# A four-sequence decoder layer on one core: a recorded order with shifted keys, a rule that keeps VectorE's two-tile steps and GpSimd's products apart, and two products moved to VectorE

## The chip, the cores and the metric

The kernel runs on one core of one Trainium2 chip. The metric is the device time of one execution in microseconds (us); before the change it is 1579.58 us, the median of three runs (1576.39 to 1582.81). The core has TensorE (PE; its weight loads are listed as PEld), VectorE (DVE), ScalarE (ACT), GpSimd (POOL) and SyncE (SP, which here only issues DMAs).

## The reference, cut to what matters

For B = 4 sequences of S = 512 tokens and 512 features, in float32, three blocks follow each other; each adds to the residual and is normalised:

```python
# 1 differential attention: 16 query heads in 8 pairs, 8 key heads in 4 groups, D = 128
p = softmax(q1 @ k1.T * D**-0.5, causal) - lam * softmax(q2 @ k2.T * D**-0.5, causal)
o = rmsnorm(p @ v) * subln_w * (1 - LAMBDA_INIT)        # v has 256 columns
x = layernorm(x + o.reshape(B, S, 1024) @ out_w.T + out_b)

# 2 a selective scan over a second input ctx (512 inner channels, 16 states)
u  = silu(causal_conv4(ctx @ in_proj.T) + conv_b)
dt = softplus(dt_proj(x_proj(u)[:16]) + dt_b);  Bm, Cm = x_proj(u)[16:]
state = state * exp(dt * A) + (dt * u) * Bm             # for each of the 512 steps
y  = (sum_n(state * Cm) + D * u) * silu(x)
x = layernorm(x + y.T)

# 3 a shared GLU and 16 routed experts on a 128-wide latent, 8 experts per token
shared = (x @ sw1.T * relu(x @ swg.T)**2) @ sw2.T
xl = x @ Wdown.T
acc = sum_e w[:, e] * ((xl @ rw1[e].T * relu(xl @ rwg[e].T)**2) @ rw2[e].T)
x = layernorm(x + shared + acc @ Wup.T)
```

Attention and the scan of a sequence don't need each other until block 2 multiplies by silu(x): the scan's input is ctx.

## The kernel before, in words

**Recording and ordering.** The kernel doesn't issue its instructions as it goes. `Notes` records every operation of every engine as a `Step` with a `key` (a due time in us that the code sets by hand as `nc.key = ...`), a cost, a lag and the steps that it depends on. `Notes.order` then lets a list of five engines run through these steps: at each event, each free engine takes, of its ready steps, the one with the smallest key, if its key is within `window` of the oldest step that is still open and its buffers are free. An ACT step that needs another function table has 10 added to its rank. The order that comes out is issued with the scheduler of the framework switched off, by one line in `Notes.trace`; this is why all instructions of the profile carry the same line, L325. On the chip each engine works through its own list in that order and waits at semaphores; the keys and costs decide the order alone.

**Vector steps beside GpSimd.** Before the change the ordering allows for an overlap of the two engines as a slowdown: a vector step that `shares` (over 256 columns and two tiles in SBUF) is made longer by a quarter of its overlap with a GpSimd `tensor_tensor`.

**Attention.** There are 16 units n (4 groups x 4 sequences), with keys from `t_unit(n) = 40 + 73.8 n`. A unit projects kT (`ps_qk` from `wk`), v (`ps_v`, evicted by VectorE, which adds the bias) and two pairs of queries (`ps_qk` from `wq`). For each of two heads and four row tiles, `softmax` makes scores `s` on PE, VectorE masks them and takes the row extreme (`e`, `nm`), ScalarE takes exp with its sum (`e`), VectorE forms `cf` and subtracts the second map from the first (`e<-e,cf`); `values` transposes (`pt`), copies (`pT`), and multiplies by v (`po`). After four tiles the output is scaled by an RMS (`rs`, a power taken on GpSimd), transposed (`pt_o`, `oT`) and projected (`ps_out`); VectorE adds the result to `res[b]`. At the start GpSimd adds the output bias to the four `res[b]` (four operations of 128x2048).

**The scan.** `scan(b)` projects ctx (`ps_in`), convolves on ScalarE and VectorE (`y`), multiplies by a sigmoid (`sgc`), projects (`ps_x`, `ps_dt`), takes the softplus in several steps (`du`, `lo`, `dt`: five 1024-column vector operations and one of the tensor-scalar kind for each half of the channels), and then takes 16 states x 2 halves. Each of these 32 steps per sequence is a vector product `h<-du,bc`, two exps on ScalarE (`da`), the hardware scan `h<-da,h`, a vector product `h<-h,bc`, and a DMA from the GpSimd queue that adds h to y in DRAM. The keys are `t_scan = SCAN + PACE * (16 b + n)`. PE does almost nothing for it, so it lies beside attention.

**Experts.** `experts(b)` loads y, forms the gate `sg` (sigmoid on ScalarE, times x on GpSimd, then `yb` times `sg` on VectorE), transposes (`pt_y`) and adds to `res[b]`, normalises, transposes (`pt_x`, `x2T`), routes (`ps_gate`, `pr`, `pt_w`), makes the latent `xl` (`ps_lat`) and the shared GLU (`pg_s`, `ph_s`). For each of 16 experts GpSimd makes `xw = xl * wb` (the latent scaled by the token's weight for that expert), and for each of two halves PE makes `pg` and `ph`, ScalarE relu and square, VectorE `ht = relu * ph`, and PE adds into `pa`. Then `ps_y`, the residual and the last normalisation.

## Time and profile before

| quantity | value |
|---|---|
| runs | 1582.81, 1579.58, 1576.39 us |
| the profiled execution | 1578.32 us, span 1576.3 us |
| granted TensorE clock, mean | 0.991 |
| PE | 1546.2 us busy (98%), 4944 instructions |
| DVE | 1159.6 us busy (74%), 1956 instructions |
| ACT | 953.2 us busy (60%), 2084 instructions |
| POOL | 307.0 us busy (19%), 288 instructions |
| DMA | 196.18 MB moved, mean 124 GB/s |

Every float32 matmul of the program is two passes of PE in the profile and every transpose one: 2112 matmuls and 720 transposes make 4944 instructions. The ends of passes are modelled in the profile, and a pass's listed duration overlaps the next pass, so times on PE are better read from start to start: a busy share of 98% doesn't say that PE ran at its peak for 98% of the span.

### The profile page before, as it was taken

The page shows a single profiled execution, that of the slowest core. Times are in us where ns is not written, and L with a number is a line of the kernel's source. Part 1 is how long each engine was busy: PE and PEld are TensorE (multiplying, and loading weights), DVE is VectorE, ACT ScalarE, POOL GpSimd, SP SyncE. Part 2 cuts the span into 40 slices and gives each one's busy share as a digit, 9 for nine tenths or more (in the row PEclk, how much of TensorE's full clock was granted, in tenths as well). Part 3 has the DMA queues.
Part 4 walks back from the last instruction along what each step waited for, and adds up shares of the span by engine and source line. Part 5 has one row for each costly group of instructions (what it writes and reads, how often), then busy time and mean ns, then how long its engine had stood idle before and what let it go on. Part 6 is the DMA issues. An engine that isn't in the chain of part 4 may idle for free.

```text
span 1576.3 us, 15893 instructions
## 1 busy us (share of the span) xinstructions
PE 1546.2 (98%) x4944; PEld 848.5 (54%) x4944; DVE 1159.6 (74%) x1956; ACT 953.2 (60%) x2084; POOL 307.0 (19%) x288
## 2 busy tenths in 40 slices
PE   7899999999999999999999999999999999999998
PEld 3465665556656555565555556655445445445443
DVE  4888897899889789988889998898883423423323
ACT  3765566686566668666565866775854444444443
POOL 4111121111121110121111121232331321320221
PEclk9899999999999999999999999999999999999999
DMA  8366683557568355666745567564771442341341
GB/s 276 90 127 118 120 165 93 107 143 133 97 131 198 65 123 120 134 111 146 168 75 123 125 147 160 118 130 94 178 162 60 138 133 78 116 128 55 118 122 53
DMA packets 105523, 196.18 MB, mean 124 GB/s; under 512 B 10896, under 2 KB 45712, under 8 KB 105440
## 3 DMA queue, kind: packets, MB, share of 16 engines
q1 hardware_dynamic: 87008, 128.06, 29.3%
q0 software_dynamic: 18432, 67.12, 24.9%
q8 instruction: 39, 0.64, 0.2%
q14 instruction: 44, 0.36, 0.1%
HBM read 119.25 MB, written 75.89 MB: 124 GB/s over the span
## 4 chain that ended last, share of the span: by engine, by line
PE 92%; DVE 4%; ACT 2%; issue 1%; DMA 0%; SPq 0%; POOLq 0%; DVEq 0%
PE ps_qk L325 20%; PE ps_out L325 13%; PE po L325 8%; PE s L325 8%; PE pa L325 7%; PE ph L325 7%; PE ps_v L325 6%; PE pg L325 6%; PE ps_y L325 3%; DVE h L325 2%; PE pt L325 2%; PE ps_in L325 2%; PE pg_s L325 2%; PE ph_s L325 2%; PE pt_o L325 2%
## 5 line engine op out<-in xcount | busy, mean ns | idle before, releaser
L325 DVE TENSOR_TENSOR_SCAN h<-da,h 128x1024 f32<-128x1024 f32 x128 | 296.9, 2319 | 3.4 <-ACT da L325 0.2
L325 POOL DMA_DIRECT2D y<-h x128 | 112.6, 880 | 779.2 <-DVE h L325 508.2
L325 PE MATMUL ps_out<-ow,oT 128*128 128x512 f32 x512 | 241.6, 593 | 0.6 <-DVE res L325 0.6
L325 PE MATMUL ps_qk<-xT,wq 128*128 128x512 f32 x512 | 238.3, 593 | 3.4 <-DVE v L325 2.2
L325 DVE TENSOR_TENSOR ht<-relu,ph 128x512 f32<-128x512 f32 x128 | 87.6, 685 | 176.1 <-ACT relu L325 87.7
L325 ACT ACTIVATE da<-dt,a_neg 128x512 f32<-128x512 f32 (+1 forms) x256 | 175.5, 716 | 33.2 <-DVE h L325 31.1
L325 ACT ACTIVATE relu<-pg 128x512 f32<-128x512 f32 x128 | 76.2, 595 | 165.3 <-PE pg L325 162.5
L325 PE MATMUL s<-kT,qT 128*128 128x384 f32 (+3 forms) x512 | 168.3, 439 | 0.2 <-DVE nm L325 0.2
L325 PE MATMUL po<-v,pT 128*128 128x256 f32 x640 | 161.2, 383 | 1.8 <-ACT pT L325 1.8
L325 DVE TENSOR_TENSOR h<-h,bc 128x1024 f32<-128x1024 f32 x128 | 158.8, 1241 | 1.4
L325 PEld LDWEIGHTS po<-v,pT 128*128 128x128 f32 x640 | 121.5, 191 | 68.7 <-issue 42.0
L325 DVE TENSOR_TENSOR h<-du,bc 128x1024 f32<-128x1024 f32 x128 | 157.8, 1233 | 0.0
L325 ACT ACTIVATE e<-e,nm 128x128 f32<-128x128 f32 (+3 forms) x256 | 141.4, 555 | 22.8 <-DVE nm L325 22.3
L325 POOL TENSOR_TENSOR xw<-xl,wb 128x512 f32<-128x512 f32 x64 | 85.9, 1343 | 285.5 <-PE ph L325 133.0
L325 DVE CUSTOM_DVE_ANT_0 e<-s,mask 128x128 f32<-128x128 f32 (+3 forms) x256 | 117.7, 486 | 25.2 <-PE s L325 24.7
L325 PEld LDWEIGHTS ps_qk<-xT,wq 128*128 128x128 f32 x512 | 92.9, 190 | 80.1 <-issue 70.9
L325 PE MATMUL ph<-xw,w_e 128*128 128x512 f32 x256 | 130.8, 593 | 2.8 <-DVE ht L325 2.8
L325 PEld LDWEIGHTS ps_out<-ow,oT 128*128 128x128 f32 x512 | 91.6, 190 | 77.2 <-issue 65.5
L325 PE MATMUL pg<-xl,w_e 128*128 128x512 f32 x256 | 130.7, 593 | 0.0
L325 PE MATMUL pa<-ht,w_e 128*128 128x512 f32 x256 | 130.3, 594 | 0.0
L325 PE MATMUL ps_v<-wv,xT 128*128 128x256 f32 x512 | 122.1, 380 | 1.2 <-DVE v L325 1.2
L325 PE MATMUL ps_qk<-xT,wk 128*128 128x512 f32 x256 | 121.0, 601 | 0.0
(120 smaller groups left out, 2087.6 us busy)
## 6 DMA issues: line engine op xcount, KB each, us to landing
y<-h POOLq DMA_DIRECT2D x128, 512.0 KB, 8.0
bc<-bc SPq DMA_DIRECT2D x64, 512.0 KB, 6.4
wb<-w SPq DMA_DIRECT2D x64, 256.0 KB, 3.6
xT<-in_xT_dram SPq DMA_DIRECT2D x15, 1024.0 KB, 7.5
w_e<-in_rwgT_dram SPq DMA_DIRECT2D x64, 128.0 KB, 2.2
w_e<-in_rw1T_dram SPq DMA_DIRECT2D x64, 128.0 KB, 2.3
w_e<-in_rw2T_dram SPq DMA_DIRECT2D x64, 128.0 KB, 2.4
wq<-in_wqkvT_dram SPq DMA_DIRECT2D x8, 512.0 KB, 7.3
```

Of the source, the lines that this page charges most:

```text
L325: getattr(getattr(self.nc, s.engine), s.name)(*[get(a) for a in s.args], **{k: get(v) for k, v in s.kw.items()})
```

## The change

Three things change.

1. **The order rule.** `shares` gets another meaning: a vector step with at least two operands in SBUF (at least one for `tensor_scalar`; reciprocal, statistics and max never count), and a GpSimd `tensor_tensor` of more than 4 columns. In `order` such a step isn't taken while another such step, of either engine, is running (`port`). The slowdown by a quarter is gone. The limit on PSUM buffers by due time is gone too (it was wide open before), and `order` takes the keys as an argument and keeps its state in local tables.
2. **The keys.** `SHIFT` adds a constant to the key of every step, by the name of the tile that it writes and the first letter of its engine: 86 of them, from -31 to +24. The base constants move too, `SCAN` from 60.47 to 140.0 above all.
3. **Two products change engine.** The gate product `sg * res` (16 of them) and the latent product `xw = xl * wb` (64) go from GpSimd to VectorE.

```diff
+SHIFT = {
+    "aT.s": 14, "a_neg.s": 8, "a_neg.v": -9, "bc.s": 7, ... "da.s": -1, ... "e.s": 8, "e.v": -1, ... "h.v": -4,
...
+}
@@ note
-        s.shares = columns(out) > 256 and sum(not v.buf.pool.psum for v in ins if columns(v) > 1) > 1
+        if engine == "vector":
+            n = 1 if name == "tensor_scalar" else 0 if name in ("reciprocal", "bn_stats", "bn_aggr", "max") else 2
+            s.shares = n > 0 and sum(not v.buf.pool.psum for v in ins) >= n
+        else:
+            s.shares = engine == "gpsimd" and name == "tensor_tensor" and columns(out) > NT
...
+        to = out.buf.name if isinstance(out, View) else s.bufs[0].name
+        s.key = self.key + SHIFT.get(to.rstrip("0123456789") + "." + engine[0], 0.0)
@@ order
+                    if s.shares and port > now:
+                        continue
...
-                if e == "vector" and best.shares:
-                    end += 0.25 * max(0.0, min(end, sharing) - now)
-                elif e == "gpsimd" and best.name == "tensor_tensor":
-                    sharing = end
+                if best.shares:
+                    port = end
@@ decoder_kernel
-    VALUES = 12.88
-    PROJECT, QUERY, SECOND = -22.47, -16.31, 20.46
-    EXPERT = [-18.73, 110.0, 228.82, 350.0]
+    VALUES = 10.71
+    PROJECT, QUERY, SECOND = -20.55, -16.82, 23.75
+    EXPERT = [-18.73, 110.0, 227.64, 350.0]
...
-    RATE, WEIGHTS, DOWN, SCALED = 5.76, 22.64, 6.95, 6.6
+    RATE, WEIGHTS, DOWN, SCALED = 5.76, 22.64, 6.39, 6.6
...
-    SCAN, PACE, CONV, SOFTPLUS = 60.47, 19.34, 70.44, 19.2
+    SCAN, PACE, CONV, SOFTPLUS = 140.0, 19.34, 70.44, 19.2
@@ experts
-            nc.gpsimd.tensor_tensor(sg, sg, res[b][:, i, :], ALU.mult)
+            nc.vector.tensor_tensor(sg, sg, res[b][:, i, :], ALU.mult)
...
-            nc.gpsimd.tensor_tensor(xw, xl, wb, ALU.mult)
+            nc.vector.tensor_tensor(xw, xl, wb, ALU.mult)
```

The list of each engine is known before the run. PE has the same 2832 steps in another order, VectorE has 80 steps more, GpSimd 80 fewer, and ScalarE's function-table loads go from 38 to 42. Everything else is the same work in another order.

More of the change, by code (lines that the diff above doesn't have):

```diff
@@ L1 @@
-import bisect
 import heapq
@@ L21 @@
 P = 128
-SLACK = 50
+ENGINES = ("tensor", "vector", "scalar", "gpsimd", "sync")
+SHIFT = {
+    "aT.s": 14, "a_neg.s": 8, "a_neg.v": -9, "bc.s": 7, "bq.s": -2, "cw.s": -2, "da.g": -4, "da.s": -1, "db.s": 3,
+    "dt.v": -12, "du.v": 20, "e.s": 8, "e.v": -1, "gb.s": -1, "h.v": -4, "ht.v": -6, "kT.s": 4, "ln_mv.v": -13,
+    "ln_nb.v": -7, "ln_rs.g": -2, "ln_st.v": 9, "ln_ve.v": 1, "lo.v": 9, "ls.v": -5, "lt.s": 6, "m.v": -4, "ms.v":
+    -4, "nlam.v": -11, "o.s": -17, "obb.s": 9, "pT.s": -3, "pa.t": 1, "pg.t": -4, "pg_s.t": -8, "ph.t": 3,
+    "ph_s.t": 3, "po.t": -10, "pr.s": -8, "pr.v": -20, "ps_gate.t": -17, "ps_in.t": -2, "ps_out.t": 5, "ps_v.t":
+    1, "ps_x.t": 11, "ps_y.t": -3, "pt_o.t": 3, "pt_w.t": -8, "pt_x.t": 4, "pt_y.t": -12, "relu.s": 23,
+    "relu_s.s": -4, "res.g": -4, "res.s": 7, "res.v": -2, "rp.v": -16, "rs.g": 6, "rs.v": -12, "sc.v": -2, "sg.s":
+    -5, "sg.v": 4, "sgc.s": 5, "sh.v": 6, "sp.v": 14, "sq.s": 4, "sub.v": -9, "v.v": 2, "w.s": 7, "wT.s": -1,
+    "w_d.s": 4, "w_dt.s": 9, "w_e.s": 24, "w_g.s": 4, "w_in.s": -31, "w_u.s": 1, "w_xp.s": 3, "x2T.s": -13,
+    "xd.s": 9, "xl.s": 3, "xm.g": 2, "xm.s": 1, "xw.v": 2, "y.g": -5, "y.s": 6, "y.v": -5, "yb.s": 6, "yb.v": 5,
+}
 B, S, HID = 4, 512, 512
@@ L139 @@
     __slots__ = (
-        "engine", "name", "args", "kw", "key", "at", "cost", "lag", "fill", "after", "left", "ready", "bufs", "table",
-        "engine_at", "shares",
+        "engine", "name", "args", "kw", "key", "at", "cost", "lag", "fill", "after", "left", "bufs", "table", "shares",
     )
@@ L192, in note @@
         s = Step()
-        s.engine, s.name, s.args, s.kw, s.key, s.at = engine, name, args, kw, self.key, len(self.steps)
+        s.engine, s.name, s.args, s.kw, s.at = engine, name, args, kw, len(self.steps)
         out = kw["out"] if "out" in kw else args[0]
@@ L200, in note @@
         s.table = {AF.Exp: "exp", AF.Sigmoid: "sigmoid", AF.Ln: "ln"}.get(args[2]) if name == "activation" else None
-        s.shares = columns(out) > 256 and sum(not v.buf.pool.psum for v in ins if columns(v) > 1) > 1
+        if engine == "vector":
[3 more added lines that the diff above has]
+            s.shares = engine == "gpsimd" and name == "tensor_tensor" and columns(out) > NT
         s.cost, s.lag, s.fill = cost(engine, name, out, rest, kw)
-        s.after, s.left, s.ready, s.bufs = [], 0, 0.0, []
+        s.after, s.left, s.bufs = [], 0, []
         before = {}
@@ L228, in touch, with order @@
             s.bufs.append(b)
-            b.uses += 1
-    def order(self, window=100.0):
-        engines = ("tensor", "vector", "scalar", "gpsimd", "sync")
-        ready = {e: [] for e in engines}
-        free_at = {e: 0.0 for e in engines}
-        events, ends, done, live = [0.0], [], [], set()
-        queue = sorted(self.steps, key=lambda s: (s.key, s.at))
-        sharing = 0.0
-        front, table, filled, landed = 0, "exp", 0.0, {e: [0.0] * 8 for e in engines}
-        seen = set()
-        for s in self.steps:
-            for b in s.bufs:
-                if id(b) not in seen:
-                    seen.add(id(b))
-                    b.key = s.key
-                    b.due = b.pool.due.setdefault(b.counts[-1], [])
-                    bisect.insort(b.due, b, key=lambda b: b.key)
-        for s in self.steps:
-            s.engine_at = None
-            if not s.left:
+    def order(self, keys, window=100.0):
+        steps, begin, finish, ready_at = self.steps, {}, {}, [0.0] * len(self.steps)
+        left = [s.left for s in steps]
+        ready = {e: [] for e in ENGINES}
+        free_at = dict.fromkeys(ENGINES, 0.0)
+        landed = {e: [0.0] * 8 for e in ENGINES}
+        events, ends, done, live, gone, took = [0.0], [], [], set(), {}, {}
+        queue = sorted(steps, key=lambda s: (keys[s.at], s.at))
+        free, due, uses = {}, {}, {}
+        for s in steps:
+            for b in s.bufs:
+                if b in uses:
+                    uses[b] += 1
+                    continue
+                uses[b] = 1
+                for c in b.counts:
+                    free[b.pool, c] = b.pool.free[c]
+                due.setdefault((b.pool, b.counts[-1]), []).append((keys[s.at], s.at, b))
+            if not left[s.at]:
                 ready[s.engine].append(s)
+        due = {c: [b for *_, b in sorted(d, key=lambda t: t[:2])] for c, d in due.items()}
+        front, table, filled, port = 0, "exp", 0.0, 0.0
         while events:
@@ L257, in order @@
             while ends and ends[0][0] <= now:
-                for b in heapq.heappop(ends)[2].bufs:
-                    b.uses -= 1
-                    if not b.uses:
+                s = heapq.heappop(ends)[2]
+                for b in s.bufs:
+                    uses[b] -= 1
+                    if not uses[b]:
                         for c in b.counts:
-                            b.pool.free[c] += 1
-            for e in engines:
+                            free[b.pool, c] += 1
+                        gone.setdefault((b.pool, b.tag), []).append(s)
+            for e in ENGINES:
                 if free_at[e] > now:
@@ L266, in order @@
                 best, least = None, None
+                most = keys[queue[front].at] + window
                 for s in ready[e]:
-                    if s.ready > now or s.key > queue[front].key + window:
+                    if ready_at[s.at] > now or keys[s.at] > most:
                         continue
@@ L271, in order @@
                         continue
-                    rank = (s.key + (10.0 if s.table not in (None, table) else 0.0), s.at)
+                    if s.shares and port > now:
+                        continue
+                    rank = (keys[s.at] + (10.0 if s.table not in (None, table) else 0.0), s.at)
                     if best is not None and rank >= least:
                         continue
-                    new = [b for b in s.bufs if id(b) not in live]
-                    if all(b.pool.free[b.tag] and b in b.due[: b.pool.free[b.counts[-1]] + SLACK * b.pool.psum] for b in new):
+                    if all(
+                        b in live
+                        or free[b.pool, b.tag]
+                        and (b.pool.psum or b in due[b.pool, b.counts[-1]][: free[b.pool, b.counts[-1]]])
+                        for b in s.bufs
+                    ):
                         best, least = s, rank
@@ L282, in order @@
                 for b in best.bufs:
-                    if id(b) not in live:
-                        live.add(id(b))
+                    if b not in live:
+                        live.add(b)
                         for c in b.counts:
-                            b.pool.free[c] -= 1
-                        b.due.remove(b)
+                            free[b.pool, c] -= 1
+                        due[b.pool, b.counts[-1]].remove(b)
+                        if gone.get((b.pool, b.tag)):
+                            took.setdefault(best.at, []).append(gone[b.pool, b.tag].pop(0))
                 end = now + best.cost
-                if e == "vector" and best.shares:
-                    end += 0.25 * max(0.0, min(end, sharing) - now)
-                elif e == "gpsimd" and best.name == "tensor_tensor":
-                    sharing = end
+                if best.shares:
+                    port = end
                 if best.table not in (None, table):
@@ L301, in order @@
                     landed[e].append(max(landed[e][-1], end + lag))
-                best.engine_at = now
+                begin[best.at], finish[best.at] = now, end + lag
                 free_at[e] = end
                 done.append(best)
-                if queue[front] is best:
-                    while front < len(queue) - 1 and queue[front].engine_at is not None:
-                        front += 1
-                    heapq.heappush(events, now)
+                while front < len(queue) - 1 and queue[front].at in begin:
+                    front += 1
+                heapq.heappush(events, now)
                 heapq.heappush(events, end)
@@ L312, in order, with trace @@
                 for s in best.after:
-                    s.left -= 1
-                    seen = end if s.engine == e and best.name != "dma_start" else end + lag
-                    s.ready = max(s.ready, seen)
-                    heapq.heappush(events, s.ready)
-                    if not s.left:
+                    left[s.at] -= 1
+                    ready_at[s.at] = max(ready_at[s.at], end if s.engine == e and best.name != "dma_start" else end + lag)
+                    heapq.heappush(events, ready_at[s.at])
+                    if not left[s.at]:
                         ready[s.engine].append(s)
+        return done, begin, finish, took
+    def trace(self):
+        done = self.order([s.key for s in self.steps])[0]
         assert len(done) == len(self.steps), "the order does not come to an end"
-        return done
-    def trace(self):
-        for s in self.order():
+        for s in done:
             get = lambda v: v.get() if isinstance(v, View) else v
```

## The prediction

> **What bounds it now.** First the page: which engine is full, and what ended last.

> ```profile
> PE 1546.2 (98%) x4944; PEld 848.5 (54%) x4944; DVE 1159.6 (74%) x1956; ACT 953.2 (60%) x2084; POOL 307.0 (19%) x288
> ...
> PE  7899999999999999999999999999999999999998
> ...
> PE 92%; DVE 4%; ACT 2%; issue 1%; DMA 0%; SPq 0%; POOLq 0%; DVEq 0%
> ```

> PE is the bound, and the change gives it the same work. So the question is what PE loses, and where. From the timeline's start times, a pass follows the one before it by 0.429 us at 512 columns, 0.322 at 384, 0.2155 at 256, 0.1095 at 128 and 0.111 at 16. With 2560, 128, 1280, 848 and 128 passes (the counts of the groups by form) that is 1098.2 + 41.2 + 275.8 + 92.9 + 14.2 = 1522 us. The first pass starts at 5.9 and the last starts 7.5 before the end; 1576.3 - 5.9 - 1522 - 7.5 leaves **41 us lost**: idle time that the page shows, and passes at half rate behind a stall. By stage I get 16.3 (0 to 118 us), 7.9 (to 1024), 15.5 (to 1182) and 1.2 (to the end), by adding each step's excess over its form's step. The windows of these stages:

> ```profile
> 0.00:118.00 118.00, 103.98 (x317) 57.63 (x318) 84.84 (x135) 69.57 (x150) 29.26 (x30) 0.96 0.60 164
> 118.00:1024.00 906.00, 904.26 (x3124) 531.75 (x3123) 798.56 (x1342) 600.55 (x1442) 141.17 (x147) 1.00 0.62 127
> 1024.00:1182.00 158.00, 151.23 (x459) 78.03 (x458) 138.89 (x205) 109.13 (x209) 53.70 (x42) 0.96 0.62 141
> 1182.00:1576.00 394.00, 386.75 (x1049) 181.11 (x1047) 137.29 (x277) 173.90 (x284) 82.86 (x69) 1.00 0.33 100
> ```

> The columns are length, then PE, PEld, DVE, ACT and POOL busy, and the granted clock. The long middle is free of loss with DVE at 88%; the clock falls to 0.96 only in the two stages that lose time; DVE is two thirds empty at the end. Then PE's own waits:

> ```profile
> PE pt L325 <- DVE e L325: 3.3, 1, 3.3
> PE ph L325 <- DVE ht L325: 2.8, 2, 1.9
> PE pt_y L325 <- DVE res L325: 2.4, 3, 0.9
> PE ps_qk L325 <- DVE v L325: 2.2, 1, 2.2
> ```

> All four are DVE being late. The timeline says why for two of them, at 30 us and at 1103 us:

> ```profile
> 27.28 2.44 DVE L325 TENSOR_SCALAR a_neg<-a_neg 128x64 f32<-128x64 f32 x1 [1.99 <-ACT a_neg L325]
> 29.64 4.51 DVE L325 TENSOR_TENSOR nlam<-ls 128x1 f32<-128x1 f32 x1
> ...
> 24.83 18.24 POOL L325 TENSOR_TENSOR res<-res,obb 128x2048 f32<-128x2048 f32 x4 [22.52 <-DMA res<-in_x_dram]
> ...
> 1103.13 1.45 POOL L325 TENSOR_TENSOR xw<-xl,wb 128x512 f32<-128x512 f32 x1
> 1103.14 3.60 DVE L325 TENSOR_TENSOR_SCAN h<-da,h 128x1024 f32<-128x1024 f32 x1
> ```

> A one-column subtraction lasts 4.51 us and ends where GpSimd's second addition ends; a scan that takes 2.32 us in its group takes 3.60 beside `xw`, and the `ht` behind it makes PE wait 1.9 us.

> **Start (16.3 us lost).** 1.7 of it are the first passes at half rate, which stay. 2.4 is the `ps_qk` behind `v`: that eviction stands behind `nlam`. In the new lists the four additions on GpSimd and `a_neg`, `nlam` on DVE keep their places, so I expect `v` at 34.3 us again; but the matmul that waits for it now stands behind 56 passes of 512 and 24 of 256 columns instead of 48 and 16: (8 x 0.429) + (8 x 0.2155) = 5.2 us more work in front, against 2.4. Hidden, with 2.8 to spare. The rest, some 9 us from 57 to 71 us and 1.3 at 96, is softplus: in the timeline DVE runs it in one piece from 49.3 to 61.2 us, and the `e` for which PE waits at 62.2 stands behind. In the new order only half of the `ps_dt` matmuls come early (44 us of PE work from the first pass), the other half at 83, and DVE's first softplus step stands behind the subtraction of the first five score tiles. Walking the new DVE list from PE's 31 us to 60 us with the group means, the transposes find `e` ready 0.6 us or more ahead. I leave 0.8 of small steps and 1.0 for waits that I didn't see: 16.3 - 1.7 - 0.8 - 1.0 = **12.8 us gained**; bounds 9 and 14.

> The first matmul comes later: `w_in` twice and three small loads stand in front of the first half of `cT`, which goes from fifth to sixth on SP, at 0.47 us from issue to issue: **0.5 us lost**.

> **Middle (7.9).** About 4 is in the form of the stream (`ps_dt`, `ps_x`, `ps_lat` follow each other by 0.51 to 0.53 us) and stays. 2.1 are two waits beside softplus at 324 and 882 us. With DVE's new list priced by the group means and set against PE's positions, these go, and one of 0.2 comes at 912. A new danger: scan 0's last products need `h` buffers back from DMAs that take 8.0 us to land, just when the next convolution holds two: up to 2 us. **1.0 gained**, between -2 and 3.

> **Transition (15.5).** GpSimd's 16 `xw` and 4 to 8 `sg` leave. What they cost DVE here: its scans, products and small steps lose 10.8 us over their usual time in this stage. What they cost on DVE: `yb<-yb,sg`, also two SBUF tiles, took 0.68 us undisturbed (mean 0.75), so the 80 products are 55 us in all, and 20 to 28 of them fall here: 14 to 19 us. So DVE has more to do in this stage. The scan adds to that: it now ends at 1150 to 1240 us of PE work instead of 1066 to 1130. By PE position and scaled to its busy time, DVE's work goes from 112 to 116 us in 1000 to 1120, with 44.7 us in the 40 from 1040, and from 45 to 101 in 1120 to 1240. The first overload, where `res` is late for `pt_y` and `pt_x`, shrinks from 5.4 to 4.0 us of backlog; the 7.7 that 1024 to 1063 lost go to 5.7. The second is new, 3.4 to 4.7: I take 4.7. The half-rate passes of 1063 to 1103 (2.2) stay. Of 1103 to 1182 (5.6) the two waits for `ht` and what followed go, 1.5 is left. 5.7 + 4.7 + 2.2 + 1.5 = 14.1, **1.4 gained**, between -9 and 9.

> [...]

> **Last stage (1.2).** DVE has 137 us of work in 394, so the other 50 or so products are hidden; the scan's tail up to 1240 makes DVE 84% full there, as in the middle. **1.0 lost**, up to 6. ScalarE's four more table loads cost 1.28 us each by their group, 5.1 us on an engine that is 60% busy: nothing, or 1.3 if one stands in front of a `pT`. In the timeline the load at 25.69 us starts where ScalarE's step before it ends, and the next step starts at 26.99. [...]

> **Sum.** 12.8 - 0.5 + 1.0 + 1.4 - 1.0 = 13.7. Span 1576.3 - 13.7 = 1562.6; what lies around the span is 2.0 (1578.32 - 1576.3), so 1564.6; the median of the runs is 1.3 above the profiled run: **1566 us**, 0.9% faster. Half a per cent, 7.9 us, is what a measurement of this kernel tells from no change.

> **Rivals.**
> - *The transition gives it back (same).* If DVE stays behind from 1024 to 1142, all three stretches lose what the first lost (7.7 in 39 us): 23 instead of 14.1, gain 4.8, 1575 us. For: 44.7 us of work in 40. [...] 0.17.
> - *Slower.* `ht` behind a scan step. In each of the 64 half-experts of the first two sequences ScalarE squares, DVE multiplies, PE adds, and DVE may be in a 2.32 us scan when `relu` is ready. If PE loses 7.7 per 39 us from 1024 to 1221, that is 38.5 against 15.1: 23.4 more, net 9.7 slower, **1589 us**. It decides from 0.21 us lost per half-expert (13.7 / 64). Against: a list priced in order shows `ht` 1 to 2 us ahead of `pa` after 1110. 0.07.
> - *The port rule does nothing at the start.* It works on the recorder's clock, not the chip's. If `v` is waited for all the same, 2.4 come back: 1568. 0.10.
> - *The transition gets better too.* [...] 0.20.
> - The forecast itself: 0.46.

> Faster holds nearly all of the forecast and two rivals: 0.75; same 0.18; slower 0.07. The range, 1553 to 1575, leaves out the slower case and half of the first rival at the top, and at the bottom a transition at its best bound beside a start at its best.

> **What would show it.** Right: no wait of PE for `v`, `e` or `pT` before 100 us, first stage at 3 to 5 us lost; `nlam` still some 4 us long; no scan over 2.4 us; DVE busy near 1200 us; PE idle near 17 us. Wrong: waits of `pa` for `ht` all through 1060 to 1240, a clock below 0.95 in several slices there, or new waits for `h` near 330 us.

## The result, and the profile after

The changed kernel took 1568.93 us, the median of 15 runs (1562.75 to 1577.64), against 1579.58 us for 15 runs of the kernel before beside it (1576.01 to 1590.58). The ratio is 0.9927, with a 95% interval of 0.9907 to 0.9947: 0.7% faster, where 1566 us (0.9% faster) had been forecast, in a range of 1553 to 1575. The profiled execution took 1571.12 us, with a span of 1569.4; it is 2.2 us above its median, and the profiled execution before is 1.3 below its own, so the two spans are only 6.9 us apart where the medians are 10.65.

The page after, the same three lines as of before:

```profile
PE 1548.7 (99%) x4944; PEld 851.2 (54%) x4944; DVE 1197.0 (76%) x2036; ACT 956.5 (61%) x2088; POOL 196.3 (13%) x208
...
PE   8999999999999999999999999999999999999998
...
PE 96%; DVE 2%; DMA 1%; ACT 1%; issue 1%; SPq 0%; POOLq 0%; DVEq 0%
```

PE's idle time (span less busy) went from 30.1 to 20.7 us, and its share of the chain that ended last from 92% to 96%. DVE took over the 80 products (1159.6 to 1197.0 us). The windows of the four stages:

```profile
0.00:118.00 118.00, 111.14 (x345) 61.87 (x346) 71.24 (x133) 69.94 (x150) 24.64 (x25) 0.99 0.43 133
118.00:1024.00 906.00, 906.00 (x3118) 534.91 (x3117) 788.14 (x1331) 600.65 (x1443) 135.72 (x144) 0.99 0.59 125
1024.00:1182.00 158.00, 153.45 (x478) 78.34 (x477) 144.19 (x233) 112.15 (x213) 21.51 (x22) 0.98 0.62 144
1182.00:1569.00 387.00, 378.11 (x1008) 176.09 (x1006) 193.38 (x342) 173.76 (x286) 14.45 (x17) 0.99 0.41 115
```

In the first stage PE is busy for 111 of 118 us instead of 104. In the middle stage and the last one the granted clock (third number from the end), which was 1.00, is now 0.99, although PE is busy for all of the middle stage. PE's waits, five of the nine lines (the others are of 0.2 to 0.7 us):

```profile
PE ps_in L352 <- DMA cT<-in_ctxT_dram: 6.3, 1, 6.3
PE pt_y L352 <- DVE res L352: 2.4, 3, 0.9
PE pa L352 <- DVE ht L352: 1.3, 2, 0.8
PE pt L352 <- ACT oT L352: 0.8, 1, 0.8
PE ps_x L352 <- DVE y L352: 0.6, 1, 0.6
```

The waits for `e` (3.3), `v` (2.2 and 1.2) and `ph` for `ht` (2.8) are gone; no single wait behind the first input is over 0.9 us.

To compare kernels, what PE loses is split in two. Each pass's distance to the next start, less its shape's step, is its excess. As much of it as a stretch of granted clock 0.5 explains (0.50 from 370.2 to 380.4 us of the changed kernel, for one; half of the overlap, and at most one step for each pass) is *half rate*, what remains above 0.13 us is *wait*, and the rest, 8 to 10 us in every kernel, is left out here. In us, of each kernel's profiled execution:

| kernel | span | half rate | waits: 0 to 118 | to 1024 | to 1182 | to the end |
|---|---|---|---|---|---|---|
| before | 1576.3 | 10.8 | 9.1 | 2.1 | 9.0 | 0.8 |
| after | 1569.4 | 14.1 | 0.9 | 0.3 | 6.7 | 3.1 |
| f1, after once more | 1565.6 | 11.2 | 0.0 | 0.2 | 7.2 | 2.1 |
| e1, products issued on GpSimd | 1560.0 | 6.3 | 0.0 | 0.0 | 6.7 | 2.3 |
| e2, before with products on VectorE | 1578.0 | 10.8 | 9.1 | 2.2 | 10.4 | 1.0 |
| e3, before with the later scan | 1593.3 | 18.3 | 0.0 | 7.5 | 20.6 | 1.8 |
| e4, after with the earlier scan | 1571.5 | 9.1 | 11.6 | 0.0 | 5.8 | 1.0 |
| e5, after without the port rule | 1564.2 | 8.7 | 1.0 | 0.2 | 7.2 | 1.9 |
| e6, after without shifts | 1570.0 | 11.1 | 2.2 | 6.3 | 4.6 | 1.0 |
| h1, scan and shifts alone | 1573.0 | 13.5 | 1.0 | 0.4 | 11.7 | 2.1 |
| e7, gate matmuls spread | 1557.7 | 5.3 | 0.9 | 0.0 | 7.0 | 1.0 |
| e8, res in quarters | 1557.3 | 4.9 | 0.0 | 0.0 | 6.6 | 1.9 |
| f4, both | 1556.3 | 4.7 | 0.6 | 0.0 | 7.0 | 1.0 |
| f3, gate matmuls twice | 1587.5 | 20.9 | 0.0 | 0.0 | 6.2 | 3.1 |

From before to after, waits fell by 10.1 us, 8.2 of them at the start. That is the first finding: the change removed waits as it should. Half rate grew by 3.3 us in this pair of profiles, but it is 11.2 in f1, the same program, against 10.8 before. The mean granted clock is 0.990 over the 47 runs of the kernel before that stand beside the experiments, and 0.992 over the 23 of the changed kernel. So the change is not shown to cost clock; this one profile had more half rate.

### The profile page after: what moved, and what is told of

Its sections match the earlier page's. It is cut to its first block, busy times and chain, and to the rows that moved or that the text cites. A ratio compares the mean times of both kernels' runs of the same rounds, so it can differ in the third digit from the quotient of the medians.

```text
span 1569.4 us, 15790 instructions
## 1 busy us (share of the span) xinstructions
PE 1548.7 (99%) x4944; PEld 851.2 (54%) x4944; DVE 1197.0 (76%) x2036; ACT 956.5 (61%) x2088; POOL 196.3 (13%) x208
## 4 chain that ended last, share of the span: by engine, by line
PE 96%; DVE 2%; DMA 1%; ACT 1%; issue 1%; SPq 0%; POOLq 0%; DVEq 0%
PE ps_qk L352 21%; PE ps_out L352 14%; PE s L352 9%; PE po L352 9%; PE ps_v L352 7%; PE pa L352 7%; PE pg L352 6%; PE ph L352 6%; PE ps_y L352 3%; PE pt L352 2%; PE pg_s L352 2%; PE ps_in L352 2%; PE ph_s L352 2%; PE pt_o L352 2%; PE ps_dt L352 1%; PE ps_lat L352 1%
## 5 line engine op out<-in xcount | busy, mean ns | idle before, releaser
L352 DVE TENSOR_TENSOR_SCAN h<-da,h 128x1024 f32<-128x1024 f32 x128 | 292.7, 2287 | 2.8
L352 PE MATMUL ps_out<-ow,oT 128*128 128x512 f32 x512 | 237.6, 595 | 0.0
L352 PEld LDWEIGHTS s<-kT,qT 128*128 128x128 f32 x512 | 90.2, 193 | 62.8 <-issue 47.6
L352 ACT COPY pT<-pt 128x128 f32<-128x128 f32 (+3 forms) x128 | 54.2, 423 | 107.6 <-PE pt L352 106.1
```

The source lines that it names most:

```text
L352: getattr(getattr(self.nc, s.engine), s.name)(*[get(a) for a in s.args], **{k: get(v) for k, v in s.kw.items()})
```

## Experiments on the four parts of the change

**The products alone (e2), on the kernel before.**

```diff
-            nc.gpsimd.tensor_tensor(sg, sg, res[b][:, i, :], ALU.mult)
+            nc.vector.tensor_tensor(sg, sg, res[b][:, i, :], ALU.mult)
...
-            nc.gpsimd.tensor_tensor(xw, xl, wb, ALU.mult)
+            nc.vector.tensor_tensor(xw, xl, wb, ALU.mult)
```

> Kernel before, its rule and keys untouched, with the latent and gate products on VectorE. Theory (start and keys made the gain; the products cost DVE about what they free): start waits 9 as before; in the transition the waits for ht go, but DVE's backlog at the first pt_y grows from 5.4 to 7.7 by the lists; time 1576 to 1582. Rival (moving the products is the whole gain): 1569 to 1573, transition waits 5 or less.

Measured: 1579.06 us (10 runs), ratio 0.9993 (0.9978 to 1.0008). By itself the move to VectorE is worth nothing that shows, as expected.

**The products back on GpSimd (e1), in the order of the changed kernel.** The order is made as if they were on VectorE; only the engine that runs them differs.

```diff
-            getattr(getattr(self.nc, s.engine), s.name)(
+            to = s.args[0].buf.name if s.args else ""
+            engine = "gpsimd" if s.engine == "vector" and to in ("xw", "sg") else s.engine
+            getattr(getattr(self.nc, engine), s.name)(
```

> Changed kernel with its order as it is, but the 64 latent and 16 gate products issued on GpSimd. Lost on PE in the profile of the changed kernel: 10.9 us in waits (0.9 / 0.3 / 6.7 / 3.1 by stage, cut at 118, 1024 and 1182 us) and 14.1 at half rate. Theory (the products on GpSimd hold up two-tile vector steps): scans of over 3 us come back between 1024 and 1182, the waits there go from 6.7 to between 9 and 12, the whole is 3 to 6 us slower than the changed kernel, about 1572 to 1575. Rival (the order alone made the gain, the engine of the products is indifferent): waits there between 6 and 8, time within 2 us of the changed kernel's 1569.

Measured: 1561.69 us (4 runs, three at 1561.51 to 1561.81 and one at 1573.32), ratio 0.9891 (0.985 to 0.9932): not slower than the changed kernel, so the theory that the products' engine matters in this order fell. The time is below what either side forecast. Two of its scans again took 3.3 us or more (3.57 and 3.30, near 1200 us; the mean of its scans is 2.305 us against 2.287), but PE waited no longer for it: 6.7 us in the transition in both kernels.

**The scan's key alone (e3), on the kernel before.**

```diff
-    SCAN, PACE, CONV, SOFTPLUS = 60.47, 19.34, 70.44, 19.2
+    SCAN, PACE, CONV, SOFTPLUS = 140.0, 19.34, 70.44, 19.2
```

> Kernel before with SCAN at 140.0 instead of 60.47 and nothing else changed. Theory (the late scan empties the start): waits before 118 us fall from 9.1 to under 2. By the lists a backlog of 8 us then stands near 904 us of PE work and one of 17 near 1011, so the whole is slower than before, 1585 to 1600. Rival (the shifts by tile cleared the start, not SCAN): 7 or more of waits before 118 us.

Measured: 1598.73 us (4 runs), ratio 1.0112 (1.0081 to 1.0143). PE's waits of the first 118 us are, in one line,

```profile
PE ps_in L325 <- DMA cT<-in_ctxT_dram: 5.9, 1, 5.9
```

so that all of the start's gain is there, and more than that is paid back later, as forecast. The span grew by 17.0 us: by 8.9 of waits and 7.5 of half rate (table). The waits of 1024 to 1182 us are led by these:

```profile
PE pt_y L325 <- DVE res L325: 4.8, 3, 2.0
PE pt L325 <- DVE res L325: 2.6, 1, 2.6
PE pt_x L325 <- ACT x2T L325: 2.5, 3, 1.1
PE ph L325 <- DVE ht L325: 2.0, 2, 1.4
```

**The scan's key taken back (e4), in the changed kernel:** the same line, from 140.0 to 60.47.

> Changed kernel with SCAN back at 60.47. Theory: the start waits come back, 8 to 13 us before some 130 us; transition waits stay at 5 to 8; time 1576 to 1583, that is, the gain is gone. Rival (shifts and products carry the gain): start waits below 3, time within 3 us of 1569.

Measured: 1572.58 us (6 runs), ratio 0.9947 (0.9925 to 0.9969). The waits of the first 118 us are back,

```profile
PE pt L352 <- DVE e L352: 3.3, 4, 1.8
PE po L352 <- ACT pT L352: 3.1, 4, 1.2
PE pt_o L352 <- ACT oT L352: 1.9, 1, 1.9
```

but the time missed its forecast of 1576 to 1583: only a part of the 10.65 us between the medians is lost, since the other stages wait 3.3 us less than in the changed kernel and half rate takes 5.0 less (table). e3 and e4 together show where the start's waits went: the scan's key takes them away, with or without the rest.

**The port rule taken out (e5).**

```diff
-                    if s.shares and port > now:
-                        continue
```

> The changed kernel without the rule that lists a GpSimd product and a two-tile vector operation apart (the `shares` test); the two products stay on VectorE, the scan's factor stays 140 and the shifts stay. My theory (the start's gain comes from the scan's later key, the rest of the order from the shifts; the port rule only moves neighbours around on paper): 1564 to 1572 us, waits of PE in the first 118 us under 2 us, summed waits of PE outside the start 8 to 12 us. Rival (the port rule is what keeps scans from being held and VectorE from being late in the middle): 1575 us or more, with scans over 2.4 us on average against 2.29 and waits of PE for h, ht or res of 5 us more than in the changed kernel.

Measured: 1561.72 us (4 runs), ratio 0.9876 (0.9848 to 0.9904). Its waits lie within 0.5 us of those of the changed kernel in the first three stages and 1.2 below in the last, and the mean scan is 2287 ns in both. The orders do differ without the rule, but with the products on VectorE nothing that the time shows hangs on it. The time is below the forecast's 1564, which the scatter of the changed kernel's own runs (f1, below) covers.

**The shifts taken out (e6).**

```diff
-        s.key = self.key + SHIFT.get(to.rstrip("0123456789") + "." + engine[0], 0.0)
+        s.key = self.key + 0.0
```

> The changed kernel with all entries of SHIFT taken as zero; the scan's factor, the port rule and the products on VectorE stay. Theory (the later scans take the start's 12 us of waits and half rate away whatever the shifts do, and the shifts pay for what the later scans cost near the end of the middle stage and in the transition): waits of PE in the first 118 us under 2 us as in the changed kernel, but a wait of 5 to 9 us near 904 us (for k and q of the next block), so 1571 to 1580 us. Rival (the shifts do nothing that the time shows, the other edits carry the gain): 1563 to 1572 us and no wait over 2 us near 904 us. Third (without the shifts the later scans cost as much as in the kernel before with only the scan's factor changed): 1590 us or more.

Measured: 1570.08 us (5 runs), ratio 0.9934 (0.9909 to 0.9958), where e5, e7 and e8 beside it took 1560.57 to 1561.72. That lies just below the theory's range and inside the rival's. The start's waits stay away but for 2.2 us. The wait that was forecast is there, at 936 us instead of 904 and 2.8 us long instead of 5 to 9; with others around it the middle stage waits 6.3:

```profile
PE ps_qk L352 <- ACT kT L352: 2.8, 1, 2.8
```

Its waits add up to 14.1 us, against 11.0 and 9.5 in the two profiles of the changed kernel: the shifts are worth some 3 to 5 us of waits, and the loss of e3 doesn't come back without them.

**Scan and shifts alone (h1):** the changed kernel with both products planned and run on GpSimd, and without the port rule.

> The changed kernel with its two products planned and issued on GpSimd as in the kernel before and without the port rule: what remains of the change is the scan's later key, the shifts and the small moves of other keys. Theory (the scan's key and the shifts are the whole gain; the products' engine and the port rule give nothing that the time shows): within 4 us of the changed kernel's time of this call, waits of PE under 2 us in the first 118 us and 7 to 10 us in the transition, the scan 2.30 to 2.33 us on average. Rival (without products on VectorE or the port rule the later scans cost as in the kernel before with only the scan's factor changed): 10 us or more above it, with 15 us or more of waits in the transition.

Measured: 1570.8 us (9 runs), ratio 0.9933 (0.9906 to 0.9961), against 1568.06 and 0.9914 (0.9881 to 0.9946) for the changed kernel beside it (f1): 2.7 us apart, with intervals that overlap. Most of the gain comes without products and port rule. Two numbers missed: the transition waits 11.7 us instead of 7 to 10, and the scan's mean is 2.34 us, with one scan of 4.59 beside `xw`. So products that are planned and run on GpSimd, without the port rule, come with 4.5 us more of waits in the transition than in f1; run there in an order that was planned for VectorE with the rule (e1) they cost none. Planned on GpSimd with the rule they were not tried.

Both e6 (no shifts) and h1 (no products, no rule) stand at 1570 us, far from e3's 1599. So neither the shifts nor the products with the rule are needed alone to avoid e3's loss. What e6 and h1 share beyond the scan's key is the small moves of other keys (`VALUES`, `PROJECT`, `QUERY`, `SECOND`, `EXPERT`, `DOWN`); no run has these alone, and their part stays open.

## Experiments on the clock

The changed kernel's trace shows what ran before three of its half-rate stretches (in the timeline's merged rows a pass count stands at the end):

```profile
367.17 2.84 PE L352 MATMUL ps_dt<-xd,w_dt 16*128 16x512 f32 x6
...
370.65 1.92 PE L352 MATMUL s<-kT,qT 128*128 128x512 f32 x2
...
1056.39 2.97 PE L352 MATMUL ps_gate<-w_g,x2T 128*128 128x16 f32 x26
...
1428.98 3.04 PE L352 MATMUL ps_gate<-w_g,x2T 128*128 128x16 f32 x26
1431.86 4.45 PE L352 MATMUL pg_s<-x2T,w_s 128*128 128x512 f32 x6
```

Two passes of `s` last 1.92 us where 1.02 is usual, and no wait stands ahead of them. The clock was halved at 370.2 us for 10.2, and at 1059.7 and 1431.7 for 3.4. Each time PE had just run about 3 us of passes that use 16 rows (`ps_dt`) or write 16 columns (`ps_gate`).

The other traces say the same. Between the clock's first rise and PE's last pass the fourteen profiles hold 52 half-rate stretches. 22 begin within 4 us behind a wait of PE. The other 30 have such passes in the 4 us before them without exception, 19 of `ps_gate` and 11 of `ps_dt`, although there are four or more such passes in the last 4 us for only some 4% of a span. But a row of passes is not enough: of the 44 rows of 26 or 32 gate passes in the eleven kernels that leave them in a row of this length, 15 were followed by half rate.

**The gate matmuls spread (e7).**

```diff
+        gate_key = nc.key
         for i in range(NT):
             for c in range(4):
+                nc.key = gate_key + 8 * (i + (c == 3))
...
+        nc.key = gate_key
```

> The changed kernel with the 32 gate matmuls of a group (16 columns each) given sort keys 8 us apart in fours, so that no 26 of them stand in a row on PE; a list of 13 becomes 4, 4, 4 and 1, and PE's order around them changes too. Theory (3 us of passes of 16 columns or rows let the clock fall to half for 3.4 us and more, though PE waits for nothing): no half-rate stretch begins behind a run of gate passes (near 1030 to 1080 or 1420 to 1470 us), the granted clock is 0.993 or more in the median run, and the time is 1563 to 1568 us; the order near 1050 us costs up to 2 us more of waits than in the changed kernel. Rival (the half-rate stretches come at random times and have nothing to do with what PE does just before): as many stretches without a wait of PE as before, clock 0.991, 1568 to 1573 us.

Measured: 1561.53 us (4 runs), ratio 0.9871 (0.9836 to 0.9906), clocks of 0.994 to 0.999. In its trace no stretch begins behind gate passes, as forecast; the one that is left, at 1031.8, stands behind PE's waits for `res`. The time is below the forecast's 1563 to 1568.

**The additions to res in quarters (e8).**

```diff
-        nc.gpsimd.tensor_tensor(res[b], res[b], obb.repeat(1, [P, NT, HID]), ALU.add)
+        for i in range(NT):
+            nc.gpsimd.tensor_tensor(res[b][:, i, :], res[b][:, i, :], obb, ALU.add)
```

> The changed kernel with each addition of the output bias to res on GpSimd (128x2048, about 4.5 us each) issued as four of 128x512. Theory (VectorE's next two-source operation is held until GpSimd's instruction ends, so its hold has the length of that instruction): the steps of VectorE at 24 to 39 us (y, a_neg, nlam), which took 5.14, 4.49 and 4.52 us, take 1.5 us or less each, v is written first by 31 us instead of 38.8, and PE gains only its 0.6 us wait for y, since PE did not wait for v: 1566 to 1572 us. Rival 1 (the hold lasts for the whole row of GpSimd operations, not for one): the three steps together still take 10 us or more. Rival 2 (these steps do bind the start): 4 us or more off the first stage's loss.

Measured: 1560.57 us (4 runs), ratio 0.9867 (0.9841 to 0.9893). The start's 0.9 us of waits are gone, but so they are in f1, which has no such edit, so this doesn't show what the edit is worth. The time is below the forecast because of half rate (4.9 against 14.1), and the gate runs are still in it. `v` came at 34.36 us instead of by 31: it then waited for PE's `ps_v`. As a test of the hold it is weaker than planned, because `y`, `a_neg` and `nlam` had begun before GpSimd did (25.24 us). The two steps that met it are longer by some 0.9 and 1.0 us, less than one quarter (19.68 / 16 = 1.23 us):

```profile
41.32 1.11 DVE L352 SCALAR_TENSOR_TENSOR cf<-l,nlam,l 128x1 f32<-128x1 f32 x1
42.46 1.32 DVE L352 SCALAR_TENSOR_TENSOR e<-e,cf 128x128 f32<-128x128 f32 x1
```

In f4, which has the same quarters, a `cf` was held for 2.79 us, over two of them. So with GpSimd instructions of 1.23 us instead of 4.73 (18.91 / 4) the steps were 0.9 to 2.6 us longer than usual, against 3.9 to 4.4 at the start of the changed kernel; but the hold was not always over one instruction.

**The changed kernel again (f1),** beside the three that follow.

> The changed kernel once more, beside the other runs of this call. Its 15 runs gave 1568.93 us at a mean granted clock of 0.991, while kernels that differ from it in little gave 1560 to 1562 us at 0.995 to 0.997 in other calls. Theory (half-rate stretches come by chance of where a stretch of small passes falls, so a kernel's runs scatter between calls): 1560 to 1570 us with clocks from 0.990 to 0.997, the time falling by about 2 us for each 0.001 of clock. Rival (the small edits of those kernels each took 7 us off): 1567 to 1571 us again and no clock over 0.995.

Measured: 1568.06 us (8 runs). Runs at a mean clock of 0.998 took 1560.06 and 1560.52 us, runs at 0.989 took 1572.65 to 1573.21: 12 to 13 us apart in the same kernel, or 1.4 us for each 0.001 of clock instead of the 2 that were forecast. Small edits that gave 1561 us in four runs are therefore not shown to be better; e1, e5, e7 and e8 have intervals that overlap with f1's.

**The gate matmuls twice (f3).**

```diff
+        for _ in range(2):
+            for i in range(NT):
+                for c in range(4):
                     nc.tensor.matmul(
                         pl[:, i * NE : (i + 1) * NE], lhsT=x2T[c][:, i * P : (i + 1) * P], rhs=w_g[:, c, :],
```

> The changed kernel with each group of gate matmuls issued twice into the same place, so that runs of 26 passes of 16 columns (3 us) become runs of 58 (6.4 us) in each of the four groups; the 128 added passes take 128 x 0.111 = 14.2 us of PE. Theory (small passes over about 3.4 us let the clock fall although PE waits for nothing; a run of 3 us does so only in some places, a run of 6.4 us always): a half-rate stretch of 3.4 us or more begins in or right behind each of the four runs, together 8 us or more of half rate outside the first 118 us and the stretches behind waits, and the time is 17 to 24 us above the changed kernel's of this call. Rival (the stretches have nothing to do with the passes): 12 to 16 us above it, and no more stretches without a wait than in the changed kernel.

Measured: 1591.14 us (10 runs), 23.1 above f1. The windows around the four runs of 58 gate passes:

```profile
1043.00:1063.00 20.00, 20.00 (x94) 13.84 (x93) 15.81 (x41) 9.27 (x15) 1.70 (x2) 0.83 0.33 58
1180.00:1200.00 20.00, 20.00 (x92) 14.65 (x93) 15.18 (x27) 9.67 (x16) 2.58 (x3) 0.76 0.75 156
1303.00:1323.00 20.00, 20.00 (x89) 14.09 (x88) 3.37 (x19) 4.23 (x8) 0.00 (x0) 0.76 0.03 10
1436.00:1456.00 20.00, 20.00 (x92) 13.97 (x91) 3.29 (x20) 4.00 (x8) 0.00 (x0) 0.83 0.07 20
```

PE is busy for all 20 us of each, and the clock is 0.76 to 0.83: in four of four rows the clock fell before the row ended or right behind it, for 6.8, 10.2, 10.2 and 6.8 us. The passes' 14.2 us and 9.7 more of half rate than in f1 (20.9 less 11.2) make 23.9, against 21.9 between the two profiled spans and 23.1 between the medians. With e7, where the rows are gone and no stretch begins behind gate passes, this settles the cause: here PE's clock falls behind small passes although it waits for nothing. Whether it is their few rows, their few columns or the weight load that each brings, no run tells apart. Nor does a run show from what length of row on the clock always falls: rows of 26 or 32 passes were followed by half rate in 15 of 44 cases, rows of 58 in four of four, and no run has a row between. The 3.4 us of the theory stand in the traces as the length of a half-rate stretch (3.41 us at 1059.7 us of the changed kernel), not as that of a row.

**Both edits (f4).**

> The changed kernel with both edits that were tried alone: gate matmuls in fours, and the additions to res on GpSimd in quarters. If the two take away different losses (half rate behind gate runs; the 0.9 us of waits in the first stage and the start's held VectorE steps): 1555 to 1559 us, at a clock of 0.996 or more. If each alone was a better call of the same kernel: within 2 us of the changed kernel's time of this call.

Measured: 1557.76 us, five runs from 1557.65 to 1558.08, ratio 0.9851 (0.9817 to 0.9885): the best of all versions, as forecast for two edits that take away different losses. All five runs lie below each of the 23 runs of the changed kernel, while the intervals of f4 and f1 just touch (0.9885 and 0.9881). Half rate is 6.5 us less than in f1 and the waits 0.9 less; what of this the quarters do is not shown. Its windows around the first two groups of gate passes:

```profile
1049.00:1069.00 20.00, 20.00 (x69) 10.53 (x68) 17.41 (x22) 9.77 (x18) 1.70 (x2) 1.00 0.50 95
1180.00:1200.00 20.00, 20.00 (x70) 10.62 (x69) 19.18 (x33) 12.77 (x21) 1.70 (x2) 1.00 0.72 160
```

## Why the prediction was right, step by step

- **Start, 12.8 gained.** Right in mechanism. No wait for `v`, `e` or `pT` before 100 us, and 8.2 of the 9.1 us of waits are gone, through the scan's key (e3, e4). Softplus is split as forecast: its first step for each half of the channels, at 49.3 and 52.5 us before, now starts at 62.7 and 102.0:

```profile
62.72 0.69 DVE L352 TENSOR_SCALAR lo<-du 128x1024 f32<-128x1024 f32 x1 [3.22 <-ACT du L352]
101.99 0.69 DVE L352 TENSOR_SCALAR lo<-du 128x1024 f32<-128x1024 f32 x1 [0.75 <-ACT du L352]
```

The stage lost 7.5 instead of the forecast 3.5. The term that was mis-sized is the 1.7 us of half rate: it was 4.4, because the clock rose at 11.8 us instead of 9.2 and fell again at 56.2 behind four `ps_dt` passes. The waits and small steps came to 3.1 instead of 1.8. Without the stretch at 56.2, in f4, the stage loses 4.5.
- **`v` at 34.3 us, hidden with 2.8 to spare.** It was hidden, but by luck. `v` came at 38.8, which is 4.5 later than forecast and more than there was to spare:

```profile
24.70 5.14 DVE L352 TENSOR_TENSOR y<-y,sgc 128x1024 f32<-128x1024 f32 x1 [0.36 <-ACT sgc L352]
29.77 4.49 DVE L352 TENSOR_SCALAR a_neg<-a_neg 128x64 f32<-128x64 f32 x1
34.18 4.52 DVE L352 TENSOR_TENSOR nlam<-ls 128x1 f32<-128x1 f32 x1
38.82 0.75 DVE L352 TENSOR_TENSOR v<-ps_v,bvb 128x256 f32<-128x256 f32 x2
...
24.26 18.91 POOL L352 TENSOR_TENSOR res<-res,obb 128x2048 f32<-128x2048 f32 x4 [21.95 <-DMA res<-in_x_dram]
```

GpSimd had begun 0.44 us before `y`, and so a third step of VectorE was held. In f1, the same program, `y` began 0.35 us before GpSimd:

```profile
24.79 1.22 DVE L352 TENSOR_TENSOR y<-y,sgc 128x1024 f32<-128x1024 f32 x1 [0.42 <-ACT sgc L352]
26.36 4.08 DVE L352 TENSOR_SCALAR a_neg<-a_neg 128x64 f32<-128x64 f32 x1 [0.34 <-ACT a_neg L352]
30.36 4.51 DVE L352 TENSOR_TENSOR nlam<-ls 128x1 f32<-128x1 f32 x1
...
25.14 18.68 POOL L352 TENSOR_TENSOR res<-res,obb 128x2048 f32<-128x2048 f32 x4 [22.83 <-DMA res<-in_x_dram]
```

The same step took 5.14 us where GpSimd had begun before it, and 1.22 us where it began before GpSimd. PE paid 0.6 us for `y`, and nothing for `v`: the matmul that needs the first `v` (done at 39.24 us) came to its turn at 39.61, some 2 us later than forecast, because PE itself was late by its first matmul, the clock and the wait for `y`. Of the 2.8 us, 0.4 were left.

- **First matmul, 0.5 lost.** 0.4 (5.9 to 6.3 us); it scatters, since e8 and f4 with the same loads started at 5.8 and 6.0.
- **Middle, 1.0 gained.** The waits fell by 1.8, but the half-rate stretch at 370 us cost 4.9, and the stage lost 2.0 more than before. f4 has the stage without it, at 5.0 lost instead of 7.9. Those 5.0 are the term that stays; of the "about 4" before, only 2.0 us stand behind `ps_dt` and `ps_x` (0.43 us is the usual step of `ps_x`), and the rest is spread over all forms.
- **Transition, 1.4 gained.** 4.2 gained, inside its bounds. The first overload was put at 5.7 and 1024 to 1063 lost 7.2: the waits for `res` there did shrink (3.2 to 1.6 us), but half rate took 3.0. 1103 to 1182 was put at 1.5 and was 1.1, with 0.5 us of waits for `ht` in place of 2.8. The new overload of 4.7 was the mis-sized term: 1063 to 1103 lost 3.0 in all, where 2.2 had stood before it. DVE's work came later than the walk over its list had it, with 34.2 us in the 40 from 1040 instead of 44.7:

```profile
1040.00:1080.00 40.00, 39.40 (x137) 21.09 (x136) 34.16 (x68) 22.58 (x43) 4.47 (x5) 0.92 0.41 80
1120.00:1240.00 120.00, 119.39 (x335) 56.58 (x334) 110.93 (x149) 72.67 (x116) 14.73 (x16) 1.00 0.71 160
```

From 1120 to 1240 us it was fuller than forecast (110.9 us busy instead of 101), and yet PE waited for it once, for 0.5 us: a full VectorE was not a wait of PE while PE's list held other work. No scan was over 2.4 us (mean 2.287).
- **Last stage, 1.0 lost.** 3.7: waits 2.3 more (0.8 of them for `ht`, 0.8 for `res`), and 1.6 of half rate behind a gate run. PE waited for no `pT` after 1182 us, so the case of a table load in front of one didn't arise. In both traces ScalarE's next step mostly starts 1.31 us after the end of the step ahead of a load (1.28 us); in the row of the prediction it is 1.30 (25.69 to 26.99 us).
- **Sum, 13.7.** The profiled span fell by 6.9 (8.8 - 0.4 - 2.0 + 4.2 - 3.7), the median by 10.65. Half rate took 3.3 of what is missing in the span; beyond the first passes and the 2.2 us of 1063 to 1103 no step had a term for it. The waits alone fell by 10.1. That the median lies within 3 us of the forecast is in part luck: the start, the middle and the last stage fell short by 9.7 us together, the transition made up 2.8, and the scatter of the runs 3.7.
- **The rivals.** "The port rule does nothing at the start" is what e5 shows (`y` takes 5.42 us there without the rule, 5.14 with it, and 1.22 in f1 with it), but the 2.4 us did not come back, because the moved matmul hides `v`. "The transition gets better too" holds in part (11.3 instead of 15.5 lost). `ht` behind a scan cost 1.3 us in two waits, not 38.5. Of the signs, DVE busy near 1200 (1197.0), `nlam` at some 4 us (4.52) and the scans were right; PE idle near 17 was 20.7, and the first stage lost 7.5 instead of 3 to 5.
- **The 80 products on VectorE.** The 14 to 19 us of VectorE's time that they were estimated to take in the transition were not lost by PE: e1, which runs them on GpSimd, and the changed kernel wait 6.7 us each there.

What stays open: why the two orders (h1 and e1) differ so much in what GpSimd's products cost, what the small moves of keys do, and in which runs a 3 us stretch of small passes halves the clock. e5 and h1 show the stretch behind `ps_dt` near 369 us as well, e7, e8 and f4 have the same six passes and show none.

## What to carry to other kernels

Where one engine is full, split its losses into waits and half rate before pricing a change of order, since half rate can hide or feign a gain: runs of f1 at a mean clock of 0.998 and of 0.989 were 12 to 13 us apart. Try not to let small matmuls stand in a row: those of 16 columns were followed by half rate here in 15 of 44 rows of 26 or 32 passes and in four of four of 58, and spreading them in fours among large ones, together with shorter GpSimd steps, took the time from 1568 to 1558 us. A due time moved by itself can be a loss (e3) and still carry the gain when the rest of the order is changed with it.
